# The bias of the softmax exponential: from a ScalarE instruction ahead of each exponential to a VectorE instruction behind each maximum

## The chip, the cores and the metric

One core of a Trainium2 chip runs the whole program. The metric is the device time of one execution in microseconds (us); smaller is better. A core has five engines that each work through an instruction stream of their own, in order: TensorE (PE; its weight loads are listed apart as PEld), VectorE (DVE), ScalarE (ACT), GpSimd (POOL) and SyncE (SP, which here only starts transfers). They wait for one another through semaphores.

## The reference

```
x = x + tanh(g_xattn) * attention(layernorm(x), ctx)       # 8 batches, 512 rows of 256
    q, k, v = layernorm(x) @ Wq, ctx @ Wk, ctx @ Wv         # 16 heads of 64; ctx is 512 x 128
    scores  = q k^T / 8
    attn    = softmax(scores)                               # over 512 keys
    out     = (attn v) @ Wo + bo
x = x + tanh(g_ffn) * moe(layernorm(x))                     # 8 experts, the best 2 of each row
```

The kernel never normalises the rows of x ahead of the projection of q. The mean is taken out of Wq beforehand, and the factor of the layer norm (one over the standard deviation of the row, with the 1/8 of the scores in it, called `rstd`) goes into the exponential: for a row, exp(rstd * s - rstd * max(s)). So the exponential has a scale, `rstd`, and a bias, `nb` = -max(s) * rstd, both one number for each of the 128 partitions. `nb` is what the change is about.

## The kernel before, in words

The attention is cut into units. A unit (b, hp, nt) is one batch, one pair of heads and one tile of 128 rows; there are 8 x 8 x 4 = 256 of them. The main loop runs over steps of two units, 128 steps, 16 to a batch. A unit goes through the engines like this:

1. `scores` (L360, PE): eight matmul records for the two units of a step, into one PSUM tile `sc` [128, 2, 512] for each unit. There are two such tiles (pool `ps_s`, two buffers), so the scores of a unit of the next step can only start when the exponential of the same-numbered unit of this step has read its tile.
2. `unit_max` (L371, DVE): one TENSOR_REDUCE gives the negated maxima `nm` [128, 2], one for each of the two heads.
3. `unit_exp`: L379 (ACT) multiplies `nm` by `rstd` into `nb` [128, 2]; L383 (ACT), once for each head, computes the exponential of 512 columns into `p`, with bias `nb` and scale `rstd`, and the sum of the row into `ss` (the accumulator's read is a record of its own in the profile).
4. `unit_norm`: L392 (DVE) takes the reciprocal `rs` of `ss`; L394 (POOL) multiplies `p` by it, once for each head, in place.
5. `unit_T` (L407, DVE, one step later): a transpose of `p` in blocks of 32 into `tt`. When the four row tiles of a pair of heads are there, `exchange` (L421) has SP start 16 transfers `pt<-tt` that complete the transposition, and `values` (L435, PE, five steps after the pair's first step) multiplies `pt` by v; ACT copies the result `av` to `ao` (L441).

`rstd` is made by POOL (L255) from statistics of DVE, five steps before the batch begins (for the first batch, ahead of the loop). The small tiles `nm`, `nb`, `ss` and `rs` have four buffers each.

Around this stand the other parts, each planned by hand: the table `SCHED` gives the step at which each part of a batch is issued (projections of q, k and v on PE with copies on ACT; `out_proj`, L453 on PE and L457 on DVE; the second layer norm; the router; experts). Six of the eight batches sort their rows by expert in two groups: DVE computes lists and places (`plan1` to `plan4`, L617 to L693), POOL fetches and scatters rows with indirect transfers (L591, L705, L764), PE multiplies the sorted rows (L734). The group of four batches does so from the sixth batch's attention on (planned at steps 80 and later), the group of two during the eighth batch's (steps 113 and later), and the last two batches compute all experts densely (L810), most of it behind the main loop.

The order of instructions on every engine is the order in which the program issues them (the scheduler of the framework is switched to manual). In a step it is: the scores of both units, the maxima of both units, and then the side work, sorted by the list `order`; in it `unit_exp0` stands second, `unit_T0` tenth, `unit_exp1` twelfth, `unit_norm0` twentieth, `unit_T1` behind the projections, `unit_norm1` later still. So on DVE each step begins with two maxima, and on ACT each unit's `nb` stands directly ahead of that unit's two exponentials.

Of the kernel before, what the change touches and what calls it, by code (L numbers as in the profile page):

```python
# [9 lines left out]
F32 = mybir.dt.float32  # L10
AF = mybir.ActivationFunctionType
ALU = mybir.AluOpType
AX = mybir.AxisListType

P = 128
# [42 lines left out]
def kernel(  # L58
# [17 lines left out]
    nc = tc.nc  # L76
# [28 lines left out]
    small = ctx.enter_context(tc.tile_pool(name="small", bufs=4))  # L105
# [15 lines left out]
    lns, xTs, qs = {}, {}, {}  # L121
# [244 lines left out]
    maxes = {}  # L366

    def unit_max(u, sc):

        nm = small.tile([P, 2], F32, tag="nm", name="nm_%d_%d_%d" % u)  # L370
        nc.vector.tensor_reduce(nm, sc, AX.X, ALU.max, negate=True)  # L371
        maxes[u] = (sc, nm)

    def unit_exp(i, u):

        sc, nm = maxes.pop(u)
        rstd = lns["q", u[0]][2][:, u[2] : u[2] + 1]
        nb = small.tile([P, 2], F32, tag="nb", name="nb_%d_%d_%d" % u)
        nc.scalar.mul(nb, nm, rstd)  # L379
        p = ppool.tile([P, 4, 2, P], F32, tag="p", name="p_%d_%d_%d" % u)  # L380
        ss = small.tile([P, 2], F32, tag="ss", name="ss_%d_%d_%d" % u)
        for j in range(2):
            nc.scalar.activation(  # L383
                p[:, :, j, :], sc[:, j, :].rearrange("p (q c) -> p q c", q=4), AF.Exp,
                bias=nb[:, j : j + 1], scale=rstd, accum_out=ss[:, j : j + 1],
            )
        probs[u] = (p, ss)
# [535 lines left out]
    for s in range(max(plan) + 1):  # L923
        side = list(plan.get(s, []))
        for i, u in enumerate(units(s)):
            side.append((unit_exp, (i, u)))
            side.append((unit_norm, (i, u)))
        for i, u in enumerate(units(s - 1)):
            side.append((unit_T, (i, u)))
            if u[2] == NT - 1:  # L930
                side.append((exchange, u[:2]))
        scs = [scores(*u) for u in units(s)]
        for u, sc in zip(units(s), scs):
            unit_max(u, sc)
        if s == 0:
            first_q(1)
            late_setup()
            add_bias(0)
        name = lambda f: f[0].__name__ + (str(f[1][0]) if f[0] in (unit_exp, unit_norm, unit_T) else "")
        for fn, args in sorted(side, key=lambda f: order[name(f)]):  # L940
            fn(*args)
# [38 lines left out]
```

## Time and profile before

| what | value |
|---|---|
| time, median of 3 runs | 1066.38 us (1063.79 to 1071.36) |
| the profiled execution: its own time | 1062.26 us |
| the profiled execution: span from the first to the last instruction | 1060.4 us |
| mean granted TensorE clock in it | 0.988 of full speed |
| `nb`, L379, ACT | 256 instructions, 292 ns each, 74.7 us in all |
| `nm`, L371, DVE | 256 instructions, 1216 ns each, 301.1 us in all |
| exponentials, L383, ACT | 512 instructions, 773 ns each, 393.8 us in all |
| `p` times `rs`, L394, POOL | 512 instructions, 701 ns each, 351.6 us in all |

How to read the profile: an engine's busy time says nothing by itself of what sets the end. The views that matter are the busy times by stage, the waits (an engine's idle time before an instruction, put down to the one that released it), the chain of waits that is followed back from the last instruction, and the timeline. A line of a group or a timeline names the line of the kernel, the engine, the operation, the tiles as out<-in, and their shapes. "x2" in a timeline means two instructions merged; "[0.50 <-ACT p L383]" is the idle time before it and its releaser. Neighbouring instructions of DVE or ACT overlap by some tens of nanoseconds in the records, so that sums of durations are a little above the time that passes.

### The profile page before, as it was taken

The numbers are of one execution on the slowest core, as the hardware profiler recorded it, in microseconds if no ns is written. First come the engines' busy times: TensorE is split into PE (matmuls) and PEld (weight loads), VectorE is DVE, ScalarE is ACT, GpSimd is POOL, SyncE is SP. The second block draws the span as 40 slices with busy tenths as digits, with TensorE's granted clock in tenths as the row PEclk, the third lists the DMA queues.
The fourth block names the chain that finished last, engine by engine and source line by source line (L and its number), as shares of the span: only waits on it lengthen the run. The fifth ranks groups of instructions, "written<-read, shape, count | busy, mean of one in ns | idle before, by whom it ended". The sixth has DMA issues, their size and how long they took to land. (4 is left out here: it accounts for less than half of the span.)

```text
span 1060.4 us, 14961 instructions
## 1 busy us (share of the span) xinstructions
PE 1015.1 (96%) x4042; PEld 495.3 (47%) x4042; DVE 805.8 (76%) x1362; ACT 654.1 (62%) x1635; POOL 586.0 (55%) x760
## 2 busy tenths in 40 slices
PE   7899999989999999999999999999999799898998
PEld 5334453534444434444444455546564345454543
DVE  4887778867888788878889966655767998584485
ACT  4787767757776677666757676565765466563000
POOL 4545436474646464745565585764736768773320
PEclk9999999999999999999999999999999899899999
DMA  7678778687776777677777877877868778687320
GB/s 254 159 189 204 184 177 190 171 156 169 180 197 128 186 188 200 135 172 189 179 179 162 211 207 188 164 178 192 207 182 170 197 197 249 178 245 191 111 91 21
DMA packets 93682, 188.94 MB, mean 178 GB/s; under 512 B 22912, under 2 KB 53280, under 8 KB 93600
## 3 DMA queue, kind: packets, MB, share of 16 engines
q1 hardware_dynamic: 85472, 171.17, 65.4%
q0 software_dynamic: 6912, 14.71, 5.9%
q10 hardware_dynamic: 1216, 2.10, 0.7%
q8 instruction: 35, 0.57, 0.2%
q14 instruction: 47, 0.39, 0.1%
HBM read 34.25 MB, written 19.42 MB: 51 GB/s over the span
## 5 line engine op out<-in xcount | busy, mean ns | idle before, releaser
L394 POOL TENSOR_SCALAR p<-p,rs 128x512 f32<-128x512 f32 x512 | 351.6, 701 | 322.7 <-DVE rs L392 306.3
L383 ACT ACTIVATE p<-sc,nb,rstd_q 128x512 f32<-128x512 f32 x512 | 393.8, 773 | 21.5 <-ACT nb L379 0.7
L371 DVE TENSOR_REDUCE nm<-sc 128x2 f32<-128x1024 f32 x256 | 301.1, 1216 | 113.2 <-PE sc L360 106.2
L407 DVE STREAM_TRANSPOSE tt<-p 128x1024 f32<-128x1024 f32 x256 | 310.9, 1229 | 4.0 <-DMA pt<-tt 2.6
L360 PE MATMUL sc<-k,q 64*128 64x512 f32 x1024 | 265.6, 633 | 17.3 <-ACT p L383 15.2
L435 PE MATMUL av<-pt,v 128*64 128x512 f32 x1024 | 234.1, 599 | 2.9 <-DMA pt<-tt 2.8
L379 ACT ACTIVATE nb<-nm,rstd_q 128x2 f32<-128x2 f32 x256 | 74.7, 292 | 207.7 <-DVE nm L371 159.5
L360 PEld LDWEIGHTS sc<-k,q 64*128 64x128 f32 x1024 | 87.3, 189 | 159.7 <-issue 70.1
L435 PEld LDWEIGHTS av<-pt,v 128*64 128x64 f32 x1024 | 68.5, 137 | 146.1 <-issue 143.0
L453 PE MATMUL po<-wo_sb,ao 128*128 128x256 f32 x512 | 125.1, 390 | 0.0
L339 PE MATMUL pq<-xT_q,wq_sb 128*128 128x512 f32 x252 | 118.5, 592 | 1.1 <-DVE x L457 1.1
L453 PEld LDWEIGHTS po<-wo_sb,ao 128*128 128x128 f32 x512 | 93.2, 190 | 51.2 <-issue 32.1
L383 ACT ACTIVATION_READ_ACCUMULATOR p<-sc,nb,rstd_q 128x1 f32 x512 | 99.2, 194 | 0.0
L705 POOL DMA_INDIRECT xg<-xn_d,rows x64 | 63.7, 995 | 14.9 <-issue 13.7
L329 PE MATMUL pv<-wv_sb,ctxT 128*128 128x256 f32 x256 | 68.9, 392 | 0.0
L764 POOL DMA_INDIRECT yg<-ysort,back x48 | 46.9, 978 | 37.8 <-DMA acc<-x1d 16.8
L734 PE MATMUL py<-we_sb,xgT 128*128 x256 | 63.0, 389 | 2.7 <-ACT xgT L726 2.7
L349 PE MATMUL pk<-ctxT,wk_sb 128*128 128x512 f32 x128 | 65.4, 592 | 0.0
L339 PEld LDWEIGHTS pq<-xT_q,wq_sb 128*128 128x128 f32 x252 | 47.8, 190 | 34.8 <-issue 30.1
L441 ACT COPY ao<-av 128x512 f32<-128x512 f32 x64 | 37.3, 583 | 43.1 <-PE av L435 32.8
L392 DVE RECIPROCAL rs<-ss 128x2 f32<-128x2 f32 x256 | 35.3, 138 | 31.6 <-ACT p L383 29.1
L329 PEld LDWEIGHTS pv<-wv_sb,ctxT 128*128 128x128 f32 x256 | 46.9, 191 | 25.7 <-issue 18.0
(126 smaller groups left out, 786.4 us busy)
## 6 DMA issues: line engine op xcount, KB each, us to landing
pt<-tt SPq DMA_DIRECT2D x1016, 128.0 KB
ysort<-y SPq DMA_DIRECT2D x32, 256.0 KB
x<-in_x SPq DMA_DIRECT2D x8, 512.0 KB
xT_q<-in_xT SPq DMA_DIRECT2D x7, 512.0 KB
xn_d<-xn_f SPq DMA_DIRECT2D x6, 512.0 KB
x1d<-x SPq DMA_DIRECT2D x5, 512.0 KB
acc<-x1d SPq DMA_DIRECT2D x20, 128.0 KB
out<-acc SPq DMA_DIRECT2D x20, 128.0 KB
```

Source lines behind the costliest of these rows:

```text
L329: nc.tensor.matmul(pv[:, r, :], lhsT=cts[b][:, ts(2 * h + r, P)], rhs=wv_sb[:, ts(g, 2 * P)], start=True, stop=True,)
L339: nc.tensor.matmul(pq, lhsT=wq_sb[:, k, ts(hp, P)], rhs=xTs["q", b][:, k, :], start=(k == 0), stop=(k == KD - 1),)
L349: nc.tensor.matmul(pk, lhsT=wk_sb[:, ts(hp, P)], rhs=cts[b], start=True, stop=True)
L360: nc.tensor.matmul(sc[:, j, :], lhsT=q[ts(j, HD), ts(nt, P)], rhs=kt[ts(j, HD), :], start=True, stop=True,)
L371: nc.vector.tensor_reduce(nm, sc, AX.X, ALU.max, negate=True)
L379: nc.scalar.mul(nb, nm, rstd)
L383: nc.scalar.activation(p[:, :, j, :], sc[:, j, :].rearrange("p (q c) -> p q c", q=4), AF.Exp, bias=nb[:, j : j + 1], scale=rstd, accum_out ...
L394: nc.gpsimd.tensor_scalar(p[:, :, j, :], p[:, :, j, :], rs[:, j : j + 1], 1.0, ALU.mult, ALU.mult)
L407: nc.vector.transpose(tts[b, hp][:, :, nt, :], p.rearrange("p q j c -> p (q j c)").rearrange("p (k l) -> p k l", l=32),)
L435: nc.tensor.matmul(av[ts(j, HD), :], lhsT=v[:, mt, c : c + HD], rhs=pt[:, :, j, mt, :], start=(mt == 0), stop=(mt == MT - 1),)
L453: nc.tensor.matmul(po, lhsT=aos[b, c][:, ts(t, P)], rhs=wo_sb[:, c, :], start=(i == 0), stop=(i == HC - 1),)
L705: nc.gpsimd.indirect_dma_start(out=xg[:, a, :], out_offset=None, in_=xn_d[g][:, :], in_offset=bass.IndirectOffsetOnAxis(ap=plans[g][1][:, ...
```

## The change

The multiplication by `rstd` is taken out of `unit_exp` and put into `unit_max`, directly behind the maximum, as a `tensor_scalar` of VectorE: `nm` times the per-partition number `rstd`, times the constant 1.0. `unit_exp` receives `nb` and `rstd` and issues only the two exponentials. Shapes, buffers and the list of side work stay as they are.

```diff
         nm = small.tile([P, 2], F32, tag="nm", name="nm_%d_%d_%d" % u)
         nc.vector.tensor_reduce(nm, sc, AX.X, ALU.max, negate=True)
-        maxes[u] = (sc, nm)
-
-    def unit_exp(i, u):
-
-        sc, nm = maxes.pop(u)
         rstd = lns["q", u[0]][2][:, u[2] : u[2] + 1]
         nb = small.tile([P, 2], F32, tag="nb", name="nb_%d_%d_%d" % u)
-        nc.scalar.mul(nb, nm, rstd)
+        nc.vector.tensor_scalar(nb, nm, rstd, 1.0, ALU.mult, ALU.mult)
+        maxes[u] = (sc, nb, rstd)
+
+    def unit_exp(i, u):
+
+        sc, nb, rstd = maxes.pop(u)
         p = ppool.tile([P, 4, 2, P], F32, tag="p", name="p_%d_%d_%d" % u)
```

## The prediction

> **What bounds the kernel now.** I read the page's table of engines first, then the busy times by stage, because averages over the whole span hide where an engine is short, then the waits, the timeline of one step, and last the chain of waits in the one stage where PE is not full.
>
> The engines:
>
> ```profile
> PE 1015.1 (96%) x4042; PEld 495.3 (47%) x4042; DVE 805.8 (76%) x1362; ACT 654.1 (62%) x1635; POOL 586.0 (55%) x760
> ```
>
> PE is busy 96% of 1060.4 us, so all that any change off PE can win is the rest, 45 us. ACT, which the change relieves, is at 62%; DVE, which it loads, is at 76%. By stage (columns: stage, its length, then PE, PEld, DVE, ACT, POOL busy, the granted clock, DMA share, GB/s):
>
> ```profile
> 0.00:60.00 60.00, 51.12 (x198) 25.08 (x200) 40.31 (x60) 38.43 (x97) 29.29 (x65) 0.97 0.77 211
> 60.00:558.00 498.00, 488.98 (x1953) 222.29 (x1952) 410.67 (x669) 349.82 (x889) 267.66 (x355) 1.00 0.76 176
> 558.00:617.00 59.00, 58.45 (x231) 27.14 (x231) 54.00 (x98) 41.58 (x106) 35.97 (x45) 1.00 0.76 191
> 617.00:810.00 193.00, 190.41 (x833) 105.74 (x829) 126.46 (x216) 126.50 (x308) 116.24 (x144) 1.00 0.77 189
> 810.00:890.00 80.00, 70.77 (x271) 33.06 (x272) 70.70 (x121) 45.21 (x114) 60.54 (x70) 0.94 0.78 196
> 890.00:965.00 75.00, 69.39 (x291) 38.56 (x291) 50.92 (x79) 46.53 (x113) 54.94 (x63) 0.93 0.78 216
> ```
>
> From 60 to 810 us PE is 98 to 99% busy. DVE is at 82% in the long second stage, 92% in the third and 88% in the fifth, where PE falls to 88%. The stage after 965 us holds no unit and isn't touched. What PE loses to the exponential, and what DVE and ACT wait for:
>
> ```profile
> PE sc L360 <- ACT p L383: 15.2, 12, 5.9
> ...
> ACT nb L379 <- DVE nm L371: 159.5, 94, 8.6
> DVE nm L371 <- PE sc L360: 106.2, 73, 8.7
> ```
>
> The scores wait for an exponential 12 times, 15.2 us in all; one of them, 5.9 us, lies in the fifth stage. The same view cut to the stages gives 5.5 us in 4 waits up to 60 us, 3.4 us in 6 from 60 to 558, 0.3 us in one from 558 to 617, none from 617 to 810. The other two lines show that ACT mostly waits for DVE's maximum, and that in 73 steps DVE is idle ahead of the maximum: in the other 55 of 128 it reaches it late, with a backlog.
>
> One step with a backlog, from the timeline (start, length):
>
> ```profile
> 303.04 2.70 POOL L394 TENSOR_SCALAR p<-p,rs 128x512 f32<-128x512 f32 x4 [2.67 <-ACT ao L441]
> ...
> 303.97 2.33 DVE L371 TENSOR_REDUCE nm<-sc 128x2 f32<-128x1024 f32 x2
> ...
> 305.20 0.30 ACT L379 ACTIVATE nb<-nm,rstd_q 128x2 f32<-128x2 f32 x1 [2.27 <-DVE nm L371]
> 305.58 0.78 ACT L383 ACTIVATE p<-sc,nb,rstd_q 128x512 f32<-128x512 f32 x1
> ...
> 307.11 0.29 ACT L379 ACTIVATE nb<-nm,rstd_q 128x2 f32<-128x2 f32 x1
> ...
> 307.48 0.78 ACT L383 ACTIVATE p<-sc,nb,rstd_q 128x512 f32<-128x512 f32 x1
> ```
>
> The reader is to see two things. An `nb` costs ACT 0.38 us (305.20 to 305.58) and 0.37 us (307.11 to 307.48) from its start to the exponential's, more than its 0.29. And POOL is multiplying a `p` at 305.2, when the first maximum ends.
>
> Last, the chain of waits from 821 us on:
>
> ```profile
> 823.41 2.30 DVE nm L371 x2
> 825.72 1.15 DVE tt L407
> 826.91 1.14 DVE tt L407
> ...
> 843.76 2.27 DVE nm L371 x2
> 846.02 1.15 DVE tt L407
> 847.22 1.15 DVE tt L407
> ```
>
> Between 821 and 866 us DVE itself is the bound, with one stretch of ACT (831.91 to 835.8) and transfers `pt<-tt` between. Here any time added to DVE is added to the end.
>
> **The change, part by part.** Removed: 256 instructions of ACT, 256 x 0.375 = 96 us of its path (74.7 us of it busy). Added: 256 instructions of DVE, each behind its maximum and ahead of the next one, and each waits for that maximum to be written. No transfer, tile or matmul is moved; the SP and POOL queues hold the same instructions.
>
> Price of one on DVE: the trace has no such multiplication of 2 elements. Nearest are the reciprocal `rs` of the same shape (L392, median 124 ns), and a TENSOR_SCALAR of 4 elements (`ve`, L251, 159 ns). I take 0.16, the row of the same operation. A dependent pair in the timeline, L504 of 0.19 us at 301.41 and L506 at 301.63, leaves 0.03 us between. So 0.19 us a unit; ends 0.12 (the reciprocal, its start hidden in the overlap) and 0.26 (the 0.07 us by which neighbours overlap is lost as well). In all 256 x 0.19 = 49 us, DVE from 806 to about 855 us.
>
> Waiting for POOL: here is the price that I trust least. A TENSOR_SCALAR of DVE and a cast, both with one source in SBUF, are seen to wait while POOL multiplies:
>
> ```profile
> 856.51 0.62 DVE L666 TENSOR_SCALAR sel<-row,part 128x24 f32<-128x24 f32 x1
> ...
> 855.71 1.39 POOL L394 TENSOR_SCALAR p<-p,rs 128x512 f32<-128x512 f32 x2 [0.49 <-DVE rs L392]
> ```
>
> `sel` has 24 elements and lasts 0.62 us; it ends at 857.13, 0.03 us behind POOL's `p`, which ends at 857.10. The casts `ai` (L568) take 0.173 us at the least and 0.334 us at the most; the four long ones again end 0.02 us behind a `p`. I laid the ends of the 256 maxima against POOL's arithmetic in the trace: 55 fall into one, and what was left of it sums to 15 us, 0.27 us each, 0.06 us a unit. Most of it, 11 us, lies between 130 and 560 us. I take 0.06 us a unit; ends 0 (2 elements might not be held) and 0.35 (half a `p`, for every unit). A longer one can't be excluded: `own` (L617) at 835.93 lasted 3.06 us, beside two of POOL's operations in a row.
>
> The Trainium skill, "SBUF — State Buffer", section "Who interferes with whom", says that a `tensor_scalar` in a two-port mode and a GpSimd instruction hold a shared port pair exclusively, the second one blocking until the first is through. That speaks against this change; the waits of `sel` agree with it, and no row here shows it for two elements. By the rule, the lock costs the 55 units their 15 us of DVE time; without it the sum below would be 1.4 us lower.
>
> What ACT's path gains in a step: in the example the first maximum ends at 303.97 + 1.215 = 305.185. Its `nb` would end at 305.375 and the exponential could start at 305.40 with the signal's 0.02 us, 0.18 us earlier than now. The second unit's pair then follows at once, 1.53 us later, 0.55 us earlier than now; its own `nb` is ready by 306.73. So the second exponential, which releases the scores' buffer, comes 0.55 us earlier where DVE is not late, and 0.17 us earlier (0.55 less two additions of 0.19) where the step starts one step's worth late.
>
> By stage:
> - 0 to 60 us: 4 waits of PE for the exponential. At most 4 x 0.55 = 2.2 us gained; one of them sits behind a late maximum. I take -1.5; ends -2.2 and 0.
> - 60 to 558 us: 6 waits, all behind late maxima: 6 x 0.17 = 1 us gained, against waits for POOL at the same places, which hold most of the 11 us. DVE has 87 us idle here for its 146 x 0.25 = 37 us. I take 0; ends -1 and +3 (six steps with half a `p` more).
> - 558 to 617 us: 16 units x 0.25 = 4.0 us on a DVE with 5.0 us idle, part of it where it can't be used. PE has only 0.55 us idle, so it is barely covered now. I take half, +2; ends 0 and +4.
> - 617 to 810 us: DVE is 66% busy and in nearly all steps waits for the scores; hidden by PE's 190.4 of 193 us. 0. If that cover were gone, 44 units would cost 11 us.
> - 810 to 890 us: 16 units on the chain x 0.25 = 4.0, less 0.55 where ACT is on it: +3.5; ends +1.4 (16 x 0.12 less 0.55) and +9.2 (16 x 0.61 less 0.55).
> - 890 to 965 us: POOL is the chain (its `p`, fetches and `xn_f`), DVE 68% busy. 0; ends -1 and +1.
>
> Sum: -1.5 + 0 + 2 + 0 + 3.5 + 0 = +4.0 us on the profiled execution's 1062.26, so 1066.3. The median of the runs shown is 4.1 us above the profiled one; so 1070.4.
>
> Queued behind the new waiting instruction: the second maximum, then the transposes `tt`, the reciprocals and the router's work. The reciprocals release POOL, the transposes release the `pt` transfers; both come up to 0.5 us later in a step. That is hidden by the three steps between a pair's last transpose and its `values`, except at the places where PE already waits for `pt` (2.8 us in two waits before 558 us). The first unit of a batch now has DVE wait for `rstd`, made five steps earlier (at 299 us for the batch that starts at 332): nothing.
>
> **The rivals.**
> - Slower by more: the wait for POOL doesn't stay at 0.06 us but becomes half a `p` on average, because DVE, running later, meets POOL's multiplications more often, and because POOL may get in twice (the 3.06 us row). For it: 28% of the first maxima already end within a `p`. Against: only 2% of the second ones do. In the third and fifth stage the sum is -1.5 - 0.55 + 32 x (0.19 + W), all on the path: it passes 10.7 us (1%) at W = 0.21 us. At W = 0.35 it is +15, and with 3 us of the second stage and the `pt` transfers that come late there, +18: 1084.5.
> - Faster (the other side): ACT's shorter path decides and DVE's additions fit in its idle time. All 11 waits before 617 us shrink by 0.55: -6 us, the fifth stage 0 because 3.2 us of its chain from 821 to 866 us are "issue", not work: 1060.4. It decides if DVE's backlog isn't longer in those steps. Against it: in 7 of the 11 the maximum itself is late. Faster by over 1% needs 10.7 us, nearly all of the 15.2 us.
> - That the change isn't done as written can be left out: the order on each engine is the program's.
>
> **How the numbers follow.** Likeliest case 0.55 (own range 1065 to 1077 from the ends above, not all at once), slower rival 0.25, faster rival 0.20. The range runs from 1058 to 1086. About 1% is what a measurement of this kernel can tell from no change, that is 1055.7 to 1077.0: the slower rival's 0.25 and a little of the likeliest's upper end make 0.28 slower; the faster rival passes 1% only in a third of its cases, 0.07; 0.65 remain.
>
> **What would show it.** `nb` on DVE at about 0.16 us where POOL is idle, and in the groups a mean of 0.2 to 0.25; its long ones ending with a `p`. ACT 75 us less busy, DVE 45 to 60 us more. In the timeline, exponentials of a step without 0.37 us between the pairs. PE's waits for the exponential smaller before 60 us, larger around 560 to 610 and 820 to 870 us. Wrong if the mean of `nb` is above 0.4 us (rival one), if PE's busy share in the third stage doesn't fall (rival two), or if `pt<-tt` appears among PE's waits with more than 10 us.

## The result, and the profile after

| | median, us | lowest to highest, us | runs |
|---|---|---|---|
| before | 1065.68 | 1063.79 to 1071.36 | 4 |
| after | 1079.55 | 1076.93 to 1086.23 | 4 |

The ratio is 1.0119, with a 95% interval of 1.0085 to 1.0153. In five more rounds later on, against 25 runs of the kernel before, the changed kernel came out at 1.0093 (1.0058 to 1.0129). The change costs about 1%; the medians differ by 8.5 and 13.9 us.

The profiled execution after took 1086.23 us (span 1084.2, mean granted clock 0.977). It is the slowest of its four, so its lines exaggerate; a second profile of the same kernel, with a span of 1071.4 us at a clock of 0.988, stands beside it wherever steps are compared. The table of engines after:

```profile
PE 1028.1 (95%) x4042; PEld 502.6 (46%) x4042; DVE 862.6 (80%) x1618; ACT 583.0 (54%) x1379; POOL 583.9 (54%) x760
```

ACT is 71 us less busy and DVE 57 us more, with 256 instructions fewer and more. The costliest groups that belong to the unit (line, engine, operation, tiles, count | busy us, mean ns of one | idle time before, releaser):

```profile
L383 ACT ACTIVATE p<-sc,nb,rstd_q 128x512 f32<-128x512 f32 x512 | 391.8, 773 | 295.9 <-DVE nb L374 211.3
...
L371 DVE TENSOR_REDUCE nm<-sc 128x2 f32<-128x1024 f32 x256 | 311.4, 1216 | 105.7 <-PE sc L360 97.2
...
L374 DVE TENSOR_SCALAR nb<-nm,rstd_q 128x2 f32<-128x2 f32 x256 | 70.8, 277 | 9.1
```

The new instruction has a mean of 0.277 us where 0.16 + 0.06 = 0.22 was predicted. ACT now waits for it where it used to wait for `nm`. The tile view of `nb` (shortest/median/longest, ns) splits the mean:

```profile
L374 DVE TENSOR_SCALAR nb<-nm,rstd_q x256: 228/228/1453, 14.2 to 980.8; 128x2 f32<-128x2 f32 x128
```

Undisturbed, one takes 0.228 us. In the trace 49 of the 256 are longer than 0.24 us; their excess is 12.4 us, or 0.05 us a unit, close to the predicted 55 hits and 0.06 us. Of the 49, 25 end within 0.035 us of the end of a `p`, and 13 of that of an indirect transfer's instruction on POOL, a kind that the prediction's 55, counted on arithmetic, leaves out. A step with such a wait, from the timeline (start, length):

```profile
306.58 2.70 POOL L394 TENSOR_SCALAR p<-p,rs 128x512 f32<-128x512 f32 x4 [2.67 <-ACT ao L441]
...
308.76 0.55 DVE L374 TENSOR_SCALAR nb<-nm,rstd_q 128x2 f32<-128x2 f32 x1
309.21 1.21 DVE L371 TENSOR_REDUCE nm<-sc 128x2 f32<-128x1024 f32 x1
...
309.43 0.78 ACT L383 ACTIVATE p<-sc,nb,rstd_q 128x512 f32<-128x512 f32 x1 [2.99 <-DVE nb L374]
...
310.46 0.23 DVE L374 TENSOR_SCALAR nb<-nm,rstd_q 128x2 f32<-128x2 f32 x1
...
310.95 0.77 ACT L383 ACTIVATE p<-sc,nb,rstd_q 128x512 f32<-128x512 f32 x1
```

The first `nb` ends at 309.31, 0.03 us behind POOL's last `p` (309.28); the maximum, 309.21, starts while that `nb` is still in the records. The second unit's exponential comes 1.52 us behind the first unit's, without a gap for an `nb`. The longest `nb`, 1.45 us at 575.87, met POOL's addition `x<-x,tgbo` (574.94 to 577.29) and ended 0.03 us behind it.

The stages, with the columns of the prediction:

```profile
0.00:60.00 60.00, 52.70 (x200) 26.27 (x202) 44.59 (x76) 34.60 (x83) 28.95 (x64) 0.97 0.76 210
60.00:558.00 498.00, 486.40 (x1934) 222.61 (x1932) 435.10 (x808) 306.55 (x737) 262.66 (x351) 0.99 0.75 175
558.00:617.00 59.00, 55.42 (x218) 25.15 (x216) 57.06 (x105) 31.41 (x76) 31.30 (x40) 1.00 0.69 169
617.00:810.00 193.00, 188.16 (x809) 104.55 (x809) 131.32 (x249) 114.54 (x263) 118.81 (x145) 0.99 0.75 185
810.00:890.00 80.00, 65.93 (x243) 29.53 (x241) 69.07 (x132) 35.85 (x88) 50.73 (x60) 0.91 0.77 176
```

These are the same times, not the same steps: step 80 starts at 553 us in the profile before and at 558 in this one. The third stage has turned over: DVE is busy 57.1 of 59 us (97%), and PE has fallen from 99% to 94%. The chain of waits, followed back from the end, now runs along DVE there (start, length):

```profile
574.71 1.13 DVE nm L371
575.87 1.45 DVE nb L374
577.32 1.14 DVE nm L371
578.71 1.15 DVE tt L407
579.90 1.14 DVE tt L407
```

PE's waits over the whole span:

```profile
PE sc L360 <- ACT p L383: 15.0, 14, 6.2
PE av L435 <- DMA pt<-tt: 9.0, 3, 3.7
PE xgt L722 <- DMA xg<-xn_d,rows: 3.4, 3, 1.3
```

The wait for the exponential is as long as before in all, 15.0 us. Cut to the stages it is 4.1 us up to 60 us (5.5 before), 1.9 us from 60 to 558 (3.4), 2.6 us in 4 waits from 558 to 617 (0.3 in one), and 6.2 us in one wait from 810 to 890 (5.9). The wait for the transfers `pt<-tt` is 9.0 us where it was 2.8. The second profiles of the two kernels (before, then after) lie closer together:

```profile
PE av L435 <- DMA pt<-tt: 5.3, 2, 3.0
```

```profile
PE av L435 <- DMA pt<-tt: 9.6, 3, 4.7
```

To lay the executions side by side, the spans were cut by hand at the first `scores` record of a step (128 steps; those planned with much side work, 80 to 91 and 110 to 120, are about the third and the fifth stage), in us:

| steps | before, two profiles | after, two profiles | difference of the means |
|---|---|---|---|
| to 8 | 59.8, 59.3 | 59.2, 57.2 | -1.3 |
| 8 to 32, 36 to 64, 68 to 80 | 441.1, 440.7 | 442.0, 440.6 | +0.3 |
| 32 to 36, 64 to 68 | 52.4, 57.1 | 56.9, 57.5 | +2.5 |
| 80 to 91 (about 555 to 640 us) | 80.5, 80.2 | 84.9, 84.8 | +4.5 |
| 91 to 110 | 168.9, 172.0 | 172.6, 169.9 | +0.8 |
| 110 to 120 (about 805 to 905 us) | 88.0, 89.2 | 94.6, 92.4 | +4.9 |
| 120 to the end | 169.8, 171.4 | 174.1, 169.0 | +0.9 |

The spans sum to 1060.4, 1070.1, 1084.2 and 1071.4. The table holds the first profile of a kernel and, behind it, the second. Two profiles of the same kernel differ by up to 5 us in a row, except in the second row and in steps 80 to 91, where they agree within 1.5 us. So +4.5 us in steps 80 to 91 stands, +4.9 us in steps 110 to 120 is likely, and the smaller differences can't be told from chance. Of steps 80 to 91, the first eight (16 units, about the third stage) take 55.2 us in both profiles before and 58.7 in both after: +3.5 us.

### The profile page after: what moved, and what is told of

Same layout as the page of the kernel before. It is cut to its first block, busy times and chain, and to the rows that moved or that the text cites. A ratio compares the mean times of both kernels' runs of the same rounds, so it can differ in the third digit from the quotient of the medians.

```text
span 1084.2 us, 14882 instructions
## 1 busy us (share of the span) xinstructions
PE 1028.1 (95%) x4042; PEld 502.6 (46%) x4042; DVE 862.6 (80%) x1618; ACT 583.0 (54%) x1379; POOL 583.9 (54%) x760
## 4 chain that ended last, share of the span: by engine, by line
PE 59%; DVE 18%; DMA 8%; SPq 4%; ACT 4%; issue 3%; POOL 3%; DVEq 0%; ACTq 0%; POOLq 0%
PE sc L360 14%; PE av L435 12%; DMA pt<-tt 8%; PE po L453 7%; DVE tt L407 7%; PE pq L339 6%; DVE nm L371 5%; PE pe L810 5%; SPq L421 4%; PE py L734 4%; PE pv L329 3%; ACT p L383 3%; PE pk L349 3%; DVE nb L374 1%; PE xgt L722 1%
## 5 line engine op out<-in xcount | busy, mean ns | idle before, releaser
L371 DVE TENSOR_REDUCE nm<-sc 128x2 f32<-128x1024 f32 x256 | 311.4, 1216 | 105.7 <-PE sc L360 97.2
L435 PE MATMUL av<-pt,v 128*64 128x512 f32 x1024 | 238.8, 609 | 9.3 <-DMA pt<-tt 9.0
L374 DVE TENSOR_SCALAR nb<-nm,rstd_q 128x2 f32<-128x2 f32 x256 | 70.8, 277 | 9.1
L441 ACT COPY ao<-av 128x512 f32<-128x512 f32 x64 | 37.6, 587 | 57.1 <-PE av L435 48.4
L734 PEld LDWEIGHTS py<-we_sb,xgT 128*128 128x128 f32 x256 | 47.7, 194 | 26.8 <-issue 15.1
```

The lines of the kernel that those rows point to most:

```text
L374: nc.vector.tensor_scalar(nb, nm, rstd, 1.0, ALU.mult, ALU.mult)
L435: nc.tensor.matmul(av[ts(j, HD), :], lhsT=v[:, mt, c : c + HD], rhs=pt[:, :, j, mt, :], start=(mt == 0), stop=(mt == MT - 1),)
L734: nc.tensor.matmul(py[:, a, :], lhsT=xt[:, k, a, :], rhs=we_sb[:, k, bass.ds(col[a], O)], start=(k == 0), stop=(k == KD - 1),)
```

## The experiments

Three theories went in. One: the loss is DVE's added time, and it lies in the two stages where DVE is nearly full (the prediction's own view, with larger sizes). Two: the wait for POOL, or transfers that come late, lose time everywhere. Three: stretches in which TensorE is granted half its clock fall anywhere and make the time. All kernels were timed in five rounds beside the kernel before on the same chip; brackets hold 95% intervals. The experiments of section 4 ran on another chip than the rest, so their rows are set beside profiles from a different chip. Where an exponential's bias is altered, it shifts all scores of a row alike, which the softmax's division takes out again.

### 1. The product on ACT in the full stages, and its complement

A step gets the new product on DVE or the old one on ACT:

```diff
+        step = 16 * u[0] + 2 * u[1] + u[2] // 2
+        on_act = 80 <= step < 91 or 110 <= step < 120     # the complement: not (...)
+        if not on_act:
             nc.vector.tensor_scalar(nb, nm, rstd, 1.0, ALU.mult, ALU.mult)
...
+        if on_act:
+            nc.scalar.mul(nb, nm, rstd)
```

> The product stays on VectorE except in steps 80 to 90 and 110 to 119 (the two stages where VectorE was 92% and 88% busy before), where ScalarE makes it as before. Theory 1 (the loss is VectorE's added time in these two stages, 4.8 + 6.6 us of the two profiles): ratio to before 0.998 to 1.004, and the two stages take what they took before. Theory 2 (the loss is spread: transfers pt<-tt that come late, at 229 to 470 us): 1.007 to 1.011. Theory 3 (half-clock stretches of TensorE that fall anywhere): about 1.012 as the change.

> The complement: the product on VectorE only in steps 80 to 90 and 110 to 119, on ScalarE elsewhere. Theory 1: 1.010 to 1.014, all of the change's loss. Theory 2: 1.000 to 1.004. Theory 3: 1.000 to 1.006, wherever the stretches fall.

Measured: 1083.38 us, ratio 1.0096 (1.0059 to 1.0133), with ACT in those steps; 1078.45 us, 1.0062 (1.0037 to 1.0087), with DVE in those steps alone. In the first, steps 80 to 91 shrink from 84.9 to 81.6 us, as they should; steps 110 to 120 don't, at 94.1 us, and the total stays where the whole change is, as theory two expected. Its profile shows where the time went instead:

```profile
PE av L440 <- DMA pt<-tt: 18.8, 7, 5.7
PE sc L360 <- ACT p L388: 14.8, 15, 5.4
```

It is the wait for the transposing transfers, 18.8 us in 7 waits; three of them, 5.7, 5.2 and 5.2 us, lie at exchanges beside or just behind a scatter of row lists (between 218 and 255, 440 and 555, 810 and 920 us; there are six such scatters in all). So the full stages can't be the whole loss. The complement has a cost of its own, 0.6%, less than theory one expected and more than theory two: they are a part. The two mixtures together cost 1.6%, more than the whole change with its 0.9 to 1.2%, though the intervals leave room for an equal sum.

### 2. Each half of the change alone

No product at all, the maximum itself as the bias:

```diff
-        nb = small.tile([P, 2], F32, tag="nb", name="nb_%d_%d_%d" % u)
-        nc.scalar.mul(nb, nm, rstd)
...
-                bias=nb[:, j : j + 1], scale=rstd, accum_out=ss[:, j : j + 1],
+                bias=nm[:, j : j + 1], scale=rstd, accum_out=ss[:, j : j + 1],
```

> The product is left out on both engines: the negated maximum without the factor is the bias (a softmax does not change when a row's bias does). It is the removal alone. If ScalarE's relief is worth what the path says (two products of 0.37 us a step, only where TensorE waits for an exponential, 15.2 us in 12 waits): 0.990 to 0.996. If the relief is hidden by TensorE everywhere: 0.997 to 1.002.

And ACT's product kept, with DVE's in addition, into a tile that nobody reads:

```diff
         nc.vector.tensor_reduce(nm, sc, AX.X, ALU.max, negate=True)
+        spare = small.tile([P, 2], F32, tag="spare", name="spare_%d_%d_%d" % u)
+        nc.vector.tensor_scalar(spare, nm, rstd, 1.0, ALU.mult, ALU.mult)
```

> The addition alone: ScalarE makes the bias as before, VectorE makes the same product into a spare tile behind each maximum. If ScalarE's relief was worth little in the change: 1.010 to 1.016, like the change. If the change's loss was a larger one that the relief partly paid back: 1.018 to 1.028.

Measured: 1067.48 us, 0.9942 (0.9912 to 0.9973), without any product; 1087.9 us, 1.0158 (1.012 to 1.0195), with both. The two halves sum to -0.58 + 1.58 = +1.0%, which is what the change costs (1.0093 and 1.0119). These two runs carry the study: the relief of ACT is real, some 6 us (3 to 9 by the interval), and DVE's 256 instructions cost some 17 us (13 to 21; the medians differ by 14.7), though nothing waits for their product. The 1.0158 lies just inside the range that was expected if the relief were worth little, but its interval reaches into the other range, and the run without any product measures the relief directly. The price is DVE's time itself: it is paid without an exponential that waits for the product.

Group of the added instruction, with both:

```profile
L373 DVE TENSOR_SCALAR spare<-nm,rstd_q 128x2 f32<-128x2 f32 x256 | 69.2, 270 | 9.1
```

and PE's waits without any product (times, longest):

```profile
PE av L433 <- DMA pt<-tt: 12.6, 3, 4.6
PE sc L360 <- ACT p L381: 10.1, 7, 5.3
```

The wait for the exponential falls from 15.2 to 10.1 us and from 12 waits to 7, steps 80 to 91 fall to 78.8 us, and the second row of the table above falls from 440.9 to 436.2 us; with both products it is 443.4 us. The 12.6 us of `pt<-tt` in a kernel that is faster than before warn against charging every such wait to the change. This is also the best version found, faster than both kernels. It needs no product because any number of the row does as a bias; what it gives up is that the largest exponent is exactly zero, so it holds for data whose rows keep exponents in range.

### 3. Both kernels again, and the wait for POOL

> The kernel before, for a profile of it on the same chip as the others of this series: ratio 1.000 within 0.003. Theory 1 (the change's loss is VectorE's time) says that TensorE's waits for pt<-tt are here about as in the profile shown first, 2.8 us; theory 2b (waits for pt<-tt at 229, 467 and 845 us belong to the chip and come with or without the change) says 8 us or more here as well.

> The changed kernel again: 1.009 to 1.015 by all theories. What tells them apart is where its profile loses time against the other one of this series: stages 558 to 617 and 810 to 890 us (theory 1), or the stretches behind waits for pt<-tt (theory 2).

Measured: 1067.28 us, 1.0005 (0.9982 to 1.0027), and 1076.0 us, 1.0093 (1.0058 to 1.0129); the profiles are those of the table. Beside them the product was replaced by a copy through a reduction over one element, and, in another kernel, by a product with two constants; both leave `rstd` out of the bias:

```diff
-        nc.vector.tensor_scalar(nb, nm, rstd, 1.0, ALU.mult, ALU.mult)
+        nc.vector.tensor_reduce(nb, nm.unsqueeze(2), AX.X, ALU.max)        # the copy
+        nc.vector.tensor_scalar(nb, nm, 0.125, 1.0, ALU.mult, ALU.mult)    # the constants
```

> Behind each maximum VectorE makes the bias by a TENSOR_REDUCE over one element, a copy without the factor: as late and as dependent as the change's product, but with no per-partition operand and of an operation that isn't seen to wait for POOL. 0.13 to 0.19 us each, none longer. If the wait for POOL (12 us in the changed kernel's profile) makes the loss: 1.000 to 1.005. If it is VectorE's time in general: 1.005 to 1.010, in proportion to its 0.16 against 0.28 us.

> The same TENSOR_SCALAR with two constants in place of the per-partition factor and 1.0 (the bias is the negated maximum times 0.125). It tells what the operand costs: 0.16 us each where POOL is idle if the 0.228 us of the change come from it, 0.228 if not; long ones beside POOL's multiplications as in the change. Time 1.006 to 1.012.

Measured: 1074.15 us, 1.0074 (1.0047 to 1.0102), for the copy; 1074.58 us, 1.0064 (1.0041 to 1.0087), for the constants. The tile views (shortest/median/longest, ns), the copy's first:

```profile
L374 DVE TENSOR_REDUCE nb<-nm x256: 154/155/157, 14.2 to 971.0; 128x2 f32<-128x2 f32 x128
```

```profile
L374 DVE TENSOR_SCALAR nb<-nm x256: 168/169/1451, 12.9 to 966.6; 128x2 f32<-128x2 f32 x128
```

Three things follow. The copy is never held by POOL: 256 instructions between 154 and 157 ns. With constants 51 are held by the same measure, more than 0.012 us above the median (39 are longer than 0.24 us). And the operand for each partition costs 0.06 us (0.228 against 0.169). The Trainium skill, "SBUF — State Buffer", section "Who interferes with whom", gives the lock on the port pair that DVE shares with GpSimd as the one source of contention between engines, names `tensor_scalar` among the operations that can take it, and says that `tensor_reduce` on trn2 never does; the product with 49 long ones of 256 and the reduction with none agree, at two elements too. But without any wait for POOL 0.74% of the 0.93% remain, though the copy is also the shortest of the three. The difference, 0.19%, lies within the two intervals, and the constants, with their waits for POOL, cost no more than the copy without. The wait for POOL is at most a small part of the loss.

### 4. Where the loss arises

ACT's product in the two full stages and at the two earlier exchanges, and the reverse, DVE's product in steps 80 to 90 alone:

```diff
+        on_act = 28 <= step < 36 or 60 <= step < 68 or 80 <= step < 91 or 108 <= step < 120
...
+        on_act = not 80 <= step < 91
```

> The product on ScalarE in steps 28 to 35, 60 to 67, 80 to 90 and 108 to 119, on VectorE elsewhere. If the loss is VectorE's time in steps 80 to 90 and, in the other three groups of steps, the transposes that come 1 us later into a stretch where pt<-tt runs beside the scatter's transfers: 0.998 to 1.003. If it is VectorE's time wherever it falls, or chance of the clock: 1.006 to 1.010, like the first of these mixtures (1.0096).

> The product on VectorE only in steps 80 to 90. The profiles show these steps 4.5 us longer with the change; so 1.004, between 1.002 and 1.006, if nothing behind them gives it back, and 0.999 to 1.002 if it is given back.

Measured: 1085.67 us, 1.0100 (1.0074 to 1.0127), for the first. If late transposes at the exchanges made the rest of the loss, it was to be 1.003 at most; it lies where "VectorE's time wherever it falls, or chance of the clock" was to put it. It gets steps 80 to 91 back to 80.3 us, the time before, and steps 110 to 120 to 90.4, and still loses as much as the whole change, elsewhere: 176.2 us in steps 91 to 110, 60.7 in the exchanges, and 445.4 in the second row, the most of all profiles. With ACT's product at the two exchanges PE still waits 4.6 and 4.2 us for `pt` there. The reverse hits: 1076.92 us, 1.0028 (1.0006 to 1.005), and steps 80 to 91 at 83.5 us. So DVE's product in these eleven steps alone costs about 3 us, 0.3%. Against the complement of section 1 (1.0062), this leaves another 0.3% for steps 110 to 120. The profiles agree in the main: these ten steps take 92.2 to 94.6 us in the six profiles with the scatter that have DVE's added instruction there, and 88.0 to 90.9 us in five that don't, the first mixture's 94.1 us left aside.

The mixtures also show what the change does ahead of step 80. Up to there the complement of section 1 and the reverse do the work of the kernel before, and the first mixture of section 1 that of the changed one. Step 80 starts at 553.3, 557.1, 559.9 and 560.6 us in the four profiles with ACT's product, and at 558.0, 555.3 and 563.6 us in the three with DVE's; PE has waited for `pt<-tt` 2.8, 5.3, 6.4 and 5.7 us until then, against 5.8, 6.8 and 13.1 us. So no loss ahead of step 80 stands out from chance, and the +2.5 us of the table's third row isn't one: that row is 57.9 and 58.8 us in the two mixtures that do the work of before. From step 80 to the end the two profiles before take 507.1 and 513.0 us, the two after 526.2 and 516.1 us.

Last, both kernels without the scatter of the row lists, whose many small transfers run beside the exchanges:

```diff
-            for t in range(NT):
-                at(b, Z["sc"] + t // 2, scatter, b, t)
```

> The kernel before with the scatter of the row lists left out (48 indirect transfers; the sorted rows are then not the right ones, the amount of the other work is the same). TensorE's waits for pt<-tt at 229 and 467 us go. 0.985 to 0.998.

> The changed kernel with the scatter left out. Against the one before without it: if the waits for pt<-tt beside the scatter make half of the change's loss, the difference shrinks from 11 us to 5 to 7 us; if they don't belong to the change, it stays at 9 to 12 us.

Measured: 1053.01 us, 0.9808 (0.9781 to 0.9835), and 1059.84 us, 0.9851 (0.982 to 0.9882). The quotient is 1.0044, the medians differ by 6.8 us; the first lies below the 0.985 that was expected at the least. PE's wait for `pt<-tt` is nearly gone, 0.3 and 1.4 us, and the exchanges' rows are alike, 48.5 and 47.9 us against 52 to 57 with the scatter. Steps 80 to 91 still lose 3.4 us and steps 110 to 120 lose 3.2 us. The loss looks about half as large without the scatter, but each of the two intervals is some 0.3% to either side, so that the factor is loose. And more than transfers goes with it: in the kernel before POOL is 50 us less busy (536 us instead of 586), and the lists stay as they were cleared, so that all fetches read one row.

## Why the prediction was right, and where it was too small

**Direction and mechanism: right in the main.** DVE's time is what costs, ACT's shorter path pays back a part, and the two stages named are those that grow. But 1079.55 us lies above the likeliest case's own 1065 to 1077, between the central 1070.4 and the slower rival's 1084.5. The range reaches that far for a rival whose cause, a longer wait for POOL, didn't come; that it held the result is partly luck.

**Price of one `nb`: too low.** 0.16 us was taken from a TENSOR_SCALAR of 4 elements; measured are 0.228 us. The row chosen lay too low by 0.07 us; the with-constants kernel shows that 0.06 of it come with the per-partition operand. From the start of the first maximum of a step to that of the second it is now 1.397 us in the median where it was 1.141: +0.26 us a unit, the upper end that the prediction gave, not 0.19.

**Wait for POOL: the size right.** 49 hits and 0.05 us a unit against 55 and 0.06, of which 13 end with an indirect transfer's instruction; that the counts agree so well is partly chance. The slower rival needed 0.21 us a unit, and is refuted.

**ACT's gain: the mechanism right, the size low.** The second unit's last exponential ends 0.41 us earlier where DVE isn't late (0.55 predicted) and about 0.15 us earlier where it is (0.17 predicted). But the sum made 2 us of it, -1.5 before 60 us and -0.55 in the fifth stage; the kernel without any product gains about 6 us.

**558 to 617 us: the step that failed most clearly.** "I take half, +2", because part of DVE's units would fit in its idle time. Little did: the eight steps of this stage grow by 3.5 us, of 16 x 0.26 = 4.2 us added, and DVE's idle time in them, 2.7 us before, is still 1.9 after. What the stage hands on adds 1 us in the next three steps. The end at +4 had been written down for just this.

**810 to 890 us: the term was +3.5.** Steps 110 to 120 show +4.9 us with the scatter and +3.2 us without; their 20 units add 20 x 0.26 = 5.2 us.

**60 to 558 us: zero in the sum, but not by the mechanism.** The steady steps come out at +0.3 us over 440. The prediction reached this by 1 us gained, set against waits for POOL, with the rest of DVE's time hidden in its idle time. Yet the kernel without any product is 4.7 us faster in these steps (436.2 us, with no half-clock stretch in them), and the one with both products 2.5 us slower (443.4). By these single profiles the zero is two larger terms that cancel: ACT's `nb` cost time where PE was 98% busy, and DVE's product costs it again. The prediction also called the later transposes hidden "except at the places where PE already waits for `pt`". That exception is what grew: the wait went from 2.8 us to 9.0 and 9.6 us in the two profiles after; but before showed 5.3 us in its second profile, and the two mixtures that do its work up to step 80 had 6.4 and 5.7 us by then, so that only the third wait, 3.2 and 2.7 us near 840 us, where both profiles before have none, stands out as the change's. `pt<-tt` didn't pass the 10 us that the prediction set as its alarm, though barely.

In sum the prediction held +6 us from DVE and -2 us from ACT, net +4; the two half-changes measure about +17 and -6. Both terms were too small by a factor of about three, which is why the net was too; that they erred alike kept the net nearer than either. About half of DVE's 17 us is placed (steps 80 to 91, steps 110 to 120), and the steady steps may hold 2.5 to 5 more. **What stays open** is the rest: the mixtures with ACT's product in the full stages got steps 80 to 91 back, but lost the time in other rows, differently in each, though the profiles of the change itself lose none ahead of step 80. Late transfers are the cause that the runs without the scatter speak for, and the mixture that spared the exchanges speaks against it; since single profiles scatter by 5 us in those rows, it is argued, not shown. Theory three doesn't make the loss: the first profile before and the second one after hold the same 23.9 us at half clock and differ by 11.0 us. The faster rival is refuted for the change as a whole and confirmed in its premise: ACT's `nb` was on the path, and without it the kernel is 0.6% faster, if nothing is put on DVE.

## What to carry to other kernels

Before an instruction is moved from one engine to another, look at the stage where the receiving engine is fullest: there nearly its whole length counted here (3.5 of 4.2 us), and idle time that is left in the stage's sum couldn't be counted on as cover. The Trainium skill, "ScalarE: Activation LUTs", section "Rules for kernel authors", advises VectorE over ScalarE for a multiplication; the instruction is indeed shorter there (0.228 us against 0.292), and the kernel is 1% slower for it, because DVE was the fuller engine (76% busy against ACT's 62%) and the bound in two stages. Better than moving a small instruction is to find that it isn't needed: here the softmax takes any shift.

## What the runs showed of the hardware

Leaving out the scatter makes the kernel before 1.9% faster (0.9808), about 20 us, though its lists are small. Some 6 us of it lie in steps 32 to 36 and 64 to 68, where its transfers run beside the exchanges and PE waits for `pt`; how much of the rest comes from POOL's 50 us or from the fetches isn't shown.

A late transfer can cost PE twice, by the wait and by a slower clock behind it. In the profile after, the chain of waits at an exchange beside the scatter (start, length):

```profile
221.71 8.92 DMA pt<-tt
...
230.65 2.55 DMA pt<-tt
...
233.21 6.64 PE av L435 x16
```

The 16 records of `av` take 6.64 us there and 3.58 elsewhere. The busy times around it (stage, length, PE, PEld, DVE, ACT, POOL, clock, DMA share, GB/s) show what goes with it:

```profile
226.00:233.00 7.00, 3.46 (x16) 1.82 (x12) 4.05 (x7) 4.85 (x13) 2.86 (x5) 0.96 0.79 151
233.00:240.00 7.00, 6.79 (x18) 2.12 (x20) 2.48 (x4) 0.11 (x1) 5.01 (x5) 0.55 0.91 208
```

In the second stretch the granted clock is 0.55; in the first profile before, both have 1.00:

```profile
226.00:233.00 7.00, 4.87 (x21) 2.39 (x22) 4.23 (x6) 6.17 (x17) 2.52 (x4) 1.00 0.85 169
233.00:240.00 7.00, 7.00 (x29) 2.98 (x26) 4.67 (x7) 2.22 (x5) 5.02 (x5) 1.00 0.76 174
```

PE waits 2.10 us for `pt` there in that profile, 3.75 us in the one after. In the twelve profiles with the scatter, at the exchanges near 233, 470 and 840 us, PE's waits for `pt` of up to 2.12 us leave the clock at full speed, and those from 2.33 us on all come with 3.4 or 6.8 us at half. This holds for these places alone: near 35 us, in the second profile before, a wait of 2.51 us keeps the full clock. The records of the clock hold 23.9 us of such half-speed stretches in the first profile before and 47.8 us in the first after, but 34.1 and 23.9 in the second ones. So they go with the first profile after being the slowest of its four (its clock is the lowest of them, 0.977), and don't explain the change.
